# Attention values by seven products in place of eight, with all engines' work ordered by a list scheduler

## The chip, the cores and the metric

The kernel runs on one core of a Trainium2 chip. The core has five engines, each with its own queue of instructions, served in order: TensorE (PE in the profile; its weight loads are PEld), VectorE (DVE), ScalarE (ACT), GpSimd (POOL) and SyncE (SP), which here only issues DMA transfers. Engines wait for each other through semaphores. The metric is the device time of one execution in microseconds.

## The reference

The input is one sequence of 2,048 rows of 256. The first half of the layer is a differential attention between two layer normalisations, the second a feed-forward with Walsh-Hadamard transforms between two more. All is float32. Cut to what matters:

```python
q, k, v = jnp.split(hidden @ Wqkv_w.T + Wqkv_b, ...)   # 16 query heads, 8 key heads, D = 128
p = softmax(causal(q0 @ k0)) - lam * softmax(causal(q1 @ k1))    # 8 pairs of query heads
o = p @ v                                     # v: 4 groups, 256 wide, each for two pairs
o = o * rsqrt(mean(o * o, -1) + EPS) * subln_w * (1 - LAMBDA_INIT)
x = x + layernorm(o.reshape(S, 2048) @ out_w.T + out_b)
h = fwht(layernorm(x) * SU_ug) / 64
h = silu(h @ W_gate.T * s1) * (h @ W_up.T * s2)                  # 1024 wide
x = x + layernorm(fwht(h * SU_dp) / 64 @ W_down.T * s3)
```

The transforms are folded into the three feed-forward weights once, inside the kernel.

## The kernel before, in words

The attention is worked group by group (4 groups of values). A group is cut in units: 8 short ones for the first 1,024 rows (128 queries each, as two halves `subs` of 64) and 16 long ones (64 queries each) for the rest. The 128 rows of a half are its 64 queries for both pairs of heads. Group 0 goes from short to long, the others from long to short.

For each unit:

- `scores` (L268): q times k for both maps, in PSUM tiles of up to 1,024 columns from a pool `ps_s` of three tiles of two banks each. VectorE moves each tile to SBUF with the running minimum (L281 with the causal mask, L286 without).
- `exponentials` (L293) on ScalarE, with the row sums.
- `combine` on VectorE: the factor `cf` (L318, L320) and then e0 + cf * e1 (L325).
- `turn` and `arrive`: VectorE transposes 32x32 blocks (L345), SP writes the result to DRAM (L350) and fetches it back in four pieces (L360), so that keys lie on partitions.
- `values` (L376): for each 128 keys one matmul of 256 columns per half, with the transposed probabilities as weights and v as the moving operand, into a pool `ps_o` of two one-bank tiles. ScalarE copies the sum out (L389) and squares it for the norm (L392); POOL makes the inverse root and scales (`inverse`, L403 to L406).
- `turn_out` and `arrive_out`: the output is transposed in the same way through DRAM (L419, L424, L434), and `project_out` (L443) multiplies it with the output weights; `accumulate` (L453) adds it to `acc` on VectorE.

The projections of q, k (`project_heads`, L181, L200 on ScalarE and L202 on VectorE) and v (`project_values`, L210, L217) use the same three pairs of banks, and so do the feed-forward's hidden products (L706) and its last ones (L741). POOL folds the transforms into the weights (`transform`, L603) between 100 and 505 us.

The order of all this is written by hand: one loop over steps, in which step k issues the scores of unit k, the combine of unit k - 1, the values of unit k - 3 and the output of units before that, with the projections, folds and feed-forward pieces put at named steps (`put`). Each engine's queue follows the order of issue.

Of the kernel before, what the change touches and what calls it, by code (L numbers as in the profile page):

```python
# [10 lines left out]
F32 = mybir.dt.float32  # L11
BF16 = mybir.dt.bfloat16
# [5 lines left out]
P = 128  # L18
# [15 lines left out]
LAG = 3  # L34
# [11 lines left out]
NCOL = 54  # L46


@with_exitstack
def kernel(  # L50
# [18 lines left out]
    ident = const.tile([P, P], F32, name="ident")  # L69
    make_identity(nc, ident)  # L70

    outb_bc = const.tile([P, HID], F32, name="outb_bc")
    make_causal_mask(nc, outb_bc[:, :P], MASKED)
    mask = const.tile([P, 1024], BF16, name="mask")
    nc.gpsimd.memset(mask[:, : 1024 - 64], 0.0)
    for p in range(2):
        nc.gpsimd.tensor_copy(mask[ts(p, 64), 1024 - 64 :], outb_bc[ts(p, 64), ts(p, 64)])
    mhalf = const.tile([P, 4], F32, name="mhalf")
    nc.gpsimd.memset(mhalf, -0.5)

    nlam = const.tile([P, 1], F32, name="nlam")

    acc = const.tile([P, NT, HID], F32, name="acc")

    def rstd_of(pool, src, n, tag):

        st = pool.tile([P, 4, 6], F32, tag="st" + tag, name="st" + tag)
        mv = pool.tile([P, 4, 2], F32, tag="mv" + tag, name="mv" + tag)
        for t in range(n):
            nc.vector.bn_stats(st[:, t, :], src[t] if isinstance(src, list) else src[:, t, :])  # L90
            nc.vector.bn_aggr(mv[:, t, :], st[:, t, :])
        ve = pool.tile([P, 4], F32, tag="ve" + tag, name="ve" + tag)
        nc.vector.tensor_scalar(ve[:, :n], mv[:, :n, 1], EPS, None, ALU.add)
        rstd = pool.tile([P, 4], F32, tag="rs" + tag, name="rs" + tag)
        nc.gpsimd.tensor_tensor(rstd[:, :n], ve[:, :n], mhalf[:, :n], ALU.pow)  # L95
        return mv, rstd
# [12 lines left out]
    x4 = x.rearrange("(b t p) d -> b p t d", p=P, t=4)  # L109

    x2 = x.rearrange("(b t s q) d -> b s q t d", t=2, s=2, q=64)
    outv = out.rearrange("(b t s q) d -> b s q t d", t=2, s=2, q=64)


    with ExitStack() as actx:
        ep = actx.enter_context(tc.tile_pool(name="ep", bufs=3))
        op = actx.enter_context(tc.tile_pool(name="op", bufs=2))
        sm = actx.enter_context(tc.tile_pool(name="sm", bufs=4))
        wop = actx.enter_context(tc.tile_pool(name="wop", bufs=1))
        qkp = actx.enter_context(tc.tile_pool(name="qkp", bufs=1))  # L120
        dram = actx.enter_context(tc.tile_pool(name="dram", bufs=4, space=bass.MemoryType.DRAM))
        ps_s = actx.enter_context(tc.tile_pool(name="ps_s", bufs=3, space=PSUM))
        ps_o = actx.enter_context(tc.tile_pool(name="ps_o", bufs=2, space=PSUM))
        actx.enter_context(tc.manual_schedule())


        qT = [qkp.tile([P, NT, 2, 2, 64], F32, name=f"q{m}") for m in range(2)]
        kT = [qkp.tile([P, S], F32, name=f"k{m}") for m in range(2)]
        vt = qkp.tile([P, NT, HID], F32, name="v")


        xstack = ExitStack()
        xtp = xstack.enter_context(tc.tile_pool(name="xtp", bufs=1, side="right"))
        xnT = xtp.tile([P, NB, 2, 512], F32, name="xnT")
        loaded = {}

        def load_qkv(g, engines, count=4):

            if g not in loaded:
                wq = xtp.tile([P, 2, 1024], F32, tag="wq", name=f"wq_{g}")  # L140
                loaded[g] = wq, xtp.tile([P, 256], F32, tag="vb", name=f"vb_{g}"), list(range(4))
            wq, _, left = loaded[g]
            for _ in range(count):
                k = left.pop(0)
                engines[k % len(engines)].dma_start(wq[:, :, ts(k, 256)], wqkv[4 * g + k])

        def load_vbias(g):
            nc.gpsimd.dma_start(loaded[g][1], vbias[:, ts(g, 256)].to_broadcast([P, 256]))

        wos = {}  # L150

        def load_wo(g):
            wo = wop.tile([P, 2, 2, HID], F32, tag="wo", name=f"wo_{g}")
            nc.gpsimd.dma_start(
                wo.rearrange("p h c o -> p (h c) o"),
                outwT[ts(g, 512), :].rearrange("(k p) o -> p k o", p=P),
            )
            wos[g] = wo

        def scale_wo(g):  # L160
            for c in range(2):
                nc.vector.tensor_scalar(
                    wos[g][:, :, c, :],
                    wos[g][:, :, c, :],
                    colv[:, C_SUBLN + c : C_SUBLN + c + 1],
                    1.0 - LAMBDA_INIT,
                    ALU.mult,
                    ALU.mult,
                )

        def project_heads(g, nb, j2, both=True, n=512):

            wq = loaded[g][0]
            cols4 = ts(nb, n)
            xb, lo = divmod(nb * n, 512)
            nt = n // P
            pp = ps_s.tile([P, 1024], F32, tag="sc", name=f"pp_{g}_{nb}_{j2}_{n}")
            for h in range(2):
                j = 2 * j2 + h
                for c in range(2):  # L180
                    nc.tensor.matmul(  # L181
                        pp[:, 512 * h : 512 * h + n],
                        lhsT=wq[:, c, ts(j, P)],
                        rhs=xnT[:, xb, c, lo : lo + n],
                        start=(c == 0),
                        stop=(c == 1),
                    )
            for h in range(2):
                j = 2 * j2 + h
                col = g * 4 + j if j < 4 else H + g * 2 + j - 4  # L190
                bias = colv[:, C_QKB + col : C_QKB + col + 1]
                src = pp[:, 512 * h : 512 * h + n]
                if j < 4:
                    dst = qT[h][:, ts(nb, nt), :, j2, :].rearrange("d t s q -> d (t s) q")
                    src = src.rearrange("d (t q) -> d t q", q=64)
                else:
                    dst = kT[h][:, cols4]
                scale = -SCALE if j < 4 else 1.0
                if h == 0 or not both:
                    nc.scalar.activation(dst, src, AF.Identity, bias=bias, scale=scale)  # L200
                else:
                    nc.vector.tensor_scalar(dst, src, scale, bias, ALU.mult, ALU.add)  # L202

        def project_values(g, nb):

            wq, vb, _ = loaded[g]
            pp = ps_s.tile([P, 1024], F32, tag="sc", name=f"pv_{g}_{nb}")
            for t in range(4):
                for c in range(2):
                    nc.tensor.matmul(  # L210
                        pp[:, ts(t, 256)],
                        lhsT=xnT[:, nb, c, ts(t, P)],
                        rhs=wq[:, c, 768:1024],
                        start=(c == 0),
                        stop=(c == 1),
                    )
            nc.vector.tensor_tensor(  # L217
                vt[:, ts(nb, 4), :],
                pp.rearrange("p (t e) -> p t e", e=256),
                vb.unsqueeze(1).to_broadcast([P, 4, 256]),  # L220
                ALU.add,
            )


        class Unit:
            def __init__(self, g, i, subs):
                self.g, self.i, self.subs = g, i, subs
                self.ns = len(subs)
                self.nk = i + 1
                self.L = [i * P + 64 * (s + 1) for s in subs]  # L230
                self.at = [a * self.nk * P for a in range(self.ns)]

                self.ng = self.nk if self.ns == 2 else (self.nk + 1) // 2
                self.n = f"{g}_{i}_{subs[0]}"

            def half(self, h):
                return [(h, 0), (h, 1)] if self.ns == 2 else [(0, h)]

            def part(self, m, a):
                return self.es[m][:, self.at[a] : self.at[a] + self.L[a]]  # L240

        def cuts(L):

            if L == 1088 or L == 1600:
                return [704, L - 704]
            return [min(1024, L - c) for c in range(0, L, 1024)]

        def begin(u):
            u.es = [ep.tile([P, S], F32, tag=f"e{m}", name=f"e{m}_{u.n}", bufs=2 + m) for m in range(2)]
            u.mx = sm.tile([P, 4, 2], F32, tag="mx", name=f"mx_{u.n}")  # L250
            u.last = sm.tile([P, 4], F32, tag="last", name=f"last_{u.n}")
            u.d = sm.tile([P, 2, 2], F32, tag="d", name=f"d_{u.n}")

        def scores(u, half):

            for a, m in u.half(half):
                k0 = 2 * a + m
                L = u.L[a]
                e = u.part(m, a)
                best = HIGHEST  # L260
                at = 0
                for c, w in enumerate(cuts(L)):
                    sc = ps_s.tile([P, 2, 512], F32, tag="sc", name=f"sc_{u.n}_{k0}_{c}")
# [65 lines left out]
        def move(u, moved):  # L329

            if u:
                turn(u)
# [695 lines left out]
```

## Time and profile before

| | |
|---|---|
| median of 3 runs | 1438.73 us (1438.65 to 1438.97) |
| the profiled execution | 1438.5 us, span 1436.7 us |
| TensorE busy | 1429.4 us, 99% |
| VectorE busy | 976.7 us, 68% |
| ScalarE busy | 503.8 us, 35% |
| POOL busy | 362.3 us, 25% |
| DMA | 210.76 MB in 501,433 packets, 66.1% of the 16 engines' span on SP's queue |

A line of groups reads: line of the kernel, engine, operation, output from inputs, shape and count, then busy us and mean ns of one, then the engine's idle time just before them and what ended it. A float32 matmul of the program shows as two records.

### The profile page before, as it was taken

The numbers are of one execution on the slowest core, as the hardware profiler recorded it, in microseconds if no ns is written. First come the engines' busy times: TensorE is split into PE (matmuls) and PEld (weight loads), VectorE is DVE, ScalarE is ACT, GpSimd is POOL, SyncE is SP. The second block draws the span as 40 slices with busy tenths as digits, with TensorE's granted clock in tenths as the row PEclk, the third lists the DMA queues.
The fourth block names the chain that finished last, engine by engine and source line by source line (L and its number), as shares of the span: only waits on it lengthen the run. The fifth ranks groups of instructions, "written<-read, shape, count | busy, mean of one in ns | idle before, by whom it ended". The sixth has DMA issues, their size and how long they took to land.

```text
span 1436.7 us, 16896 instructions
## 1 busy us (share of the span) xinstructions
PE 1429.4 (99%) x5436; PEld 1042.5 (73%) x5436; DVE 976.7 (68%) x1789; ACT 503.8 (35%) x1114; POOL 362.3 (25%) x684
## 2 busy tenths in 40 slices
PE   9999999999999999999999999999999999999998
PEld 7567777656766777776677776676777777888887
DVE  6588787847556777544867678445776788656774
ACT  3453433323133334323433334323424445531111
POOL 2037725830028821011111111111111121121110
PEclk9999999999999999999999999999999999999999
DMA  5379899856667897832798887631999999732110
GB/s 147 74 176 201 190 183 222 175 89 139 154 135 145 166 208 179 165 86 62 156 184 178 172 199 168 129 81 52 208 204 192 193 196 188 173 91 81 52 56 18
DMA packets 501433, 210.76 MB, mean 147 GB/s; under 512 B 396032, under 2 KB 499456, under 8 KB 501216
## 3 DMA queue, kind: packets, MB, share of 16 engines
q1 hardware_dynamic: 498128, 200.73, 66.1%
q0 software_dynamic: 2352, 8.26, 2.1%
q8 instruction: 44, 0.72, 0.2%
q10 hardware_dynamic: 864, 0.68, 0.2%
q14 instruction: 45, 0.37, 0.1%
HBM read 111.05 MB, written 98.57 MB: 146 GB/s over the span
## 4 chain that ended last, share of the span: by engine, by line
PE 99%; DMA 0%; DVE 0%; POOL 0%; issue 0%; ACT 0%; POOLq 0%; DVEq 0%
PE po L376 33%; PE sc L268 32%; PE pp L181 11%; PE gu L706 8%; PE pout L443 8%; PE pd L741 4%; PE pv L210 4%; DMA vb<-in_vbias 0%; PE warm L479 0%; DVE v L217 0%; PE pst L508 0%; ACT q L200 0%; POOL lt L536 0%; DVE stx L90 0%; POOL rsx L95 0%
## 5 line engine op out<-in xcount | busy, mean ns | idle before, releaser
L376 PE MATMUL po<-v,pt 128*128 128x256 f32 x2176 | 488.0, 379 | 0.0
L268 PE MATMUL sc<-k,q 128*128 128x512 f32 (+11 forms) x1280 | 477.6, 519 | 0.3 <-DVE last L281 0.2
L376 PEld LDWEIGHTS po<-v,pt 128*128 128x128 f32 x2176 | 426.5, 196 | 66.5 <-issue 18.3
L268 PEld LDWEIGHTS sc<-k,q 128*128 128x128 f32 x1280 | 240.7, 190 | 200.1 <-issue 156.7
L293 ACT ACTIVATE e<-e,last 128x192 f32<-128x192 f32 (+28 forms) x256 | 298.9, 1169 | 199.4 <-DVE last L281 181.8
L286 DVE TENSOR_SCALAR_CACHE_REDUCE e<-sc 128x1024 f32<-128x1024 f32 (+1 forms) x128 | 149.2, 1166 | 153.3 <-PE sc L268 153.3
L389 ACT COPY osb<-po 128x256 f32<-128x256 f32 (+1 forms) x96 | 42.6, 443 | 483.4 <-PE po L376 482.5
L403 POOL TENSOR_TENSOR u<-ss,ed 128x1 f32<-128x1 f32 (+1 forms) x96 | 20.0, 208 | 750.1 <-ACT po L392 749.9
L325 DVE SCALAR_TENSOR_TENSOR e<-e,cf,e 128x64 f32<-128x64 f32 (+31 forms) x128 | 174.1, 1381 | 3.4
L345 DVE STREAM_TRANSPOSE e<-e 128x1536 f32<-128x1536 f32 (+7 forms) x96 | 166.6, 1735 | 7.1
L181 PE MATMUL pp<-xnT,wq 128*128 128x512 f32 (+1 forms) x408 | 170.7, 568 | 0.1
L281 DVE CUSTOM_DVE_ANT_0 e<-sc,mask 128x64 f32<-128x64 f32 (+15 forms) x128 | 89.2, 718 | 79.9 <-PE sc L268 78.7
L181 PEld LDWEIGHTS pp<-xnT,wq 128*128 128x128 f32 x408 | 77.0, 190 | 79.2 <-issue 76.1
L281 DVE CUSTOM_DVE_ANT_0 e<-sc,mask,mx 128x384 f32<-128x384 f32 (+13 forms) x128 | 105.7, 826 | 23.8 <-PE sc L268 8.4
L443 PE MATMUL pout<-wo,oT 128*128 128x256 f32 x512 | 120.9, 379 | 0.0
L443 PEld LDWEIGHTS pout<-wo,oT 128*128 128x128 f32 x512 | 97.3, 190 | 12.8
L719 ACT ACTIVATE hT<-gu,colv 128x256 f32<-128x256 f32 x64 | 26.8, 470 | 120.9 <-PE gu L706 120.8
L706 PE MATMUL gu<-fxnT,wgate 128*128 128x256 f32 x256 | 65.8, 379 | 0.0
L706 PE MATMUL gu<-fxnT,wup 128*128 128x256 f32 x256 | 65.7, 379 | 0.0
L406 POOL TENSOR_SCALAR osb<-osb,f 128x256 f32<-128x256 f32 x128 | 62.5, 488 | 11.9
L404 POOL TENSOR_TENSOR f<-u,mhalf 128x1 f32<-128x1 f32 (+1 forms) x96 | 58.3, 608 | 7.5
L725 DVE SCALAR_TENSOR_TENSOR hT<-gu,colv,hT 128x256 f32<-128x256 f32 x64 | 30.6, 478 | 41.0 <-ACT hT L719 41.0
(100 smaller groups left out, 1079.5 us busy)
## 6 DMA issues: line engine op xcount, KB each, us to landing
dr<-e SPq DMA_DIRECT2D x20, 1024.0 KB, 4.7
pt<-dr SPq DMA_DIRECT2D x80, 256.0 KB, 5.7
dr<-e SPq DMA_DIRECT2D x20, 896.0 KB, 4.5
pt<-dr SPq DMA_DIRECT2D x80, 224.0 KB, 5.1
do<-xo SPq DMA_DIRECT2D x64, 256.0 KB, 3.8
oT<-do SPq DMA_DIRECT2D x256, 64.0 KB, 2.6
dr<-e SPq DMA_DIRECT2D x20, 768.0 KB, 4.3
pt<-dr SPq DMA_DIRECT2D x80, 192.0 KB, 4.5
```

Of the source, the lines that this page charges most:

```text
L181: nc.tensor.matmul(pp[:, 512 * h : 512 * h + n], lhsT=wq[:, c, ts(j, P)], rhs=xnT[:, xb, c, lo : lo + n], start=(c == 0), stop=(c == 1),)
L268: nc.tensor.matmul(src[:, k, :], lhsT=qT[m][:, u.i, u.subs[a]].rearrange("d p q -> d (p q)"), rhs=kT[m][:, lo : lo + w // n], start=True, ...
L281: nc.vector.tensor_tensor_reduce(dst, src, msk, 1.0, best, ALU.add, ALU.min, accum_out=u.last[:, k0 : k0 + 1])
L286: nc.vector.tensor_scalar(dst, src, 1.0, best, ALU.mult, ALU.min, accum_out=least)
L293: nc.scalar.activation(e, e, AF.Exp, bias=u.last[:, 2 * a + m : 2 * a + m + 1], scale=-1.0, accum_out=u.d[:, a, m : m + 1],)
L325: nc.vector.scalar_tensor_tensor(e0, e1, cf[:, a : a + 1], e0, ALU.mult, ALU.add)
L345: nc.vector.transpose(x[:, : 256 * ng].rearrange("p (g c r) -> p r g c", g=ng, r=2), e[:, : 256 * ng].rearrange(order, g=ng, r=2),)
L376: nc.tensor.matmul(u.po[:, ts(a, HID)], lhsT=ptv[:, g, r, :], rhs=vt[:, kc, :], start=(kc == 0), stop=(kc == u.i),)
L404: nc.gpsimd.tensor_tensor(f[:, : u.ns], w[:, : u.ns], mhalf[:, : u.ns], ALU.pow)
L406: nc.gpsimd.tensor_scalar(u.osb[:, a, :], u.osb[:, a, :], f[:, a : a + 1], 16.0, ALU.mult, ALU.mult)
L443: nc.tensor.matmul(u.pout[:, :HID], lhsT=u.oT[:, c, p, :], rhs=wos[u.g][:, p, c, :], start=(p == 0 and c == 0), stop=(p == 1 and c == 1),)
L706: nc.tensor.matmul(ps[:, ts(2 * j + n, 256)], lhsT=ffn[which][:, c, ts(fc, P)], rhs=xnT[:, c, :], start=(c == 0), stop=(c == 1),)
```

## The change

**Values.** The probabilities of one block (256 queries for two pairs of heads, 512 rows) and 256 keys are one item. In the items off the diagonal the product of [2 x 2] blocks is made with seven products in place of eight (Strassen's scheme): POOL makes four sums of blocks of the transposed probabilities per item (`sums`) and, per group, four differences of blocks of v (`vm`). Now v or its differences are the weights and the probabilities the moving operand, so the result comes with the value's 256 entries on partitions and the queries in columns. Diagonal items keep their six products. The products add up in four banks of their own over a block's items; at the end of a block they are collected by ScalarE, VectorE and POOL (`collect_tasks`).

**Output.** Because the result is already turned, `turn_out` and `arrive_out` go. The norm's sum runs over partitions now: squares on ScalarE, a half-sum on POOL, a transpose and a reduction on VectorE, a small round trip through DRAM, a last reduction, and the inverse root on POOL. The factor is applied after the output projection, on ScalarE and VectorE, and POOL adds to `acc`, which starts as the output's bias.

**Evictions.** All q and k evictions are on ScalarE, the pads too.

**PSUM.** Two tiles of two banks (`pair`) serve scores, projections, output projections, the first four feed-forward blocks and all its last products; the four other banks hold the value sums and, once the last block is collected, the hidden products of the last four feed-forward blocks.

**Order.** Every piece of work is a `Task` with an engine, a cost, a key (smaller goes first), dependencies, a latency and perhaps a PSUM slot. `Plan.run` plays the tasks through on costs that are written in the code and issues each when its engine takes it there. Combines and transposes are cut in two for each unit; value fetches go by item.

```diff
+class Plan:
+    def run(self):
+        engines = sorted({t.engine for t in self.tasks})
+        free = dict.fromkeys(engines, 0.0)
...
+        while count < len(self.tasks):
+            best = None
+            for e in engines:
...
+                options = []
+                for k, (_, _, t) in enumerate(sorted(ready[e], key=lambda r: r[:2])):
+                    at = max(first, t.ready, self.room(t)[0])
+                    options.append((at, k, t))
+                    if at == first:
+                        break
...
+    ps_s = ctx.enter_context(tc.tile_pool(name="ps_s", bufs=1, space=PSUM))
+    ps_z = ctx.enter_context(tc.tile_pool(name="ps_z", bufs=1, space=PSUM))
...
+    plan = Plan({"pair": 2, "zb": 4, "sq": 1, "y": 2})
+    def t_pe(n, cols):
+        return n * (cols / 600 + 0.005)
+    def t_dve(cols, fixed=0.15):
+        return fixed + cols / 960
...
+        mixed = add(DVE, t_dve(hi - lo, 0.34), n + MIX + 0.25 * k, c, cf)
+        turned = add(DVE, t_dve(256 * (g1 - g0)), n + MIX + 0.5 + 0.25 * k, t, mixed, u.padded)
...
+        def sums(k):
+            s1, s2, s3, s4 = (b.s[j][:, k, :].rearrange("p (u h c) -> p u h c", u=4, h=2) for k in range(4))
+            a11, a12, a21, a22 = (b.p[j][:, r, k] for r in range(2) for k in range(2))
+            args = (
+                (s1, a21, a22, ALU.add),
+                (s2, s1, a11, ALU.subtract),
+                (s4, a12, s2, ALU.subtract),
+                (s3, a11, a21, ALU.subtract),
+            )[k]
+            nc.gpsimd.tensor_tensor(*args)
...
+            ss.append(add(POOL, 0.8, key + SUM_KEY + 0.01 * k, lambda k=k: sums(k), fetched, room if k == 0 else ss[-1]))
+        def first():
+            p, v = b.p[j], vv[:, j]
+            product(b, 0, 0, v[:, 0, 0, :], p[:, 0, 0], end)
+            product(b, 2, 0, v[:, 1, 0, :], p[:, 0, 1], False)
+            product(b, 2, 256, vm[:, j, 3, :], p[:, 1, 1], False)
+        def second():
+            s = b.s[j]
+            product(b, 1, 0, vm[:, j, 0, :], s[:, 0, :], end)
+            product(b, 0, 256, vm[:, j, 1, :], s[:, 1, :], end)
+        def third():
+            s = b.s[j]
+            product(b, 3, 0, vv[:, j, 1, 1, :], s[:, 3, :], False)
+            product(b, 1, 256, vm[:, j, 2, :], s[:, 2, :], end)
...
+            def cu():
+                nc.vector.tensor_tensor(w["w"][:, 2, :], b.z[0][:, 256:], w["w"][:, 0, :], ALU.add)
+            def co0():
+                nc.vector.tensor_tensor(
+                    b.o[:, 0], b.z[2].rearrange("p (r q) -> p r q", r=2), w["w"][:, 0::3, :], ALU.add
+                )
...
+            def y1(t=t):
+                nc.vector.scalar_tensor_tensor(
+                    r["y", t], r["p"][:, t, HID:], b.f[:, 2 * t + 1 : 2 * t + 2], r["y", t], ALU.mult, ALU.add
+                )
+            def ac(t=t):
+                a = acc[:, 2 * b.i + t, :]
+                nc.gpsimd.tensor_tensor(a, r["y", t], a, ALU.add)
...
+                if many == 2:
+                    r["p"] = pair(where, f"gu_{b}_{k}")
+                else:
+                    r["p"] = ps_z.tile([P, 1, 512], F32, tag=f"z{where}", name=f"gu_{b}_{k}")
```

## The prediction

> **What bounds the kernel now.** I read the page's busy shares, clock row and chain first. TensorE is busy 99% of the span at full clock and carries 99% of the chain; every other engine has slack.
>
> ```profile
> PE 1429.4 (99%) x5436; PEld 1042.5 (73%) x5436; DVE 976.7 (68%) x1789; ACT 503.8 (35%) x1114; POOL 362.3 (25%) x684
> PEclk9999999999999999999999999999999999999999
> PE 99%; DMA 0%; DVE 0%; POOL 0%; issue 0%; ACT 0%; POOLq 0%; DVEq 0%
> ```
>
> Busy is not the same as dense, so next the chain in order of time, and the tail of the timeline.
>
> ```profile
> 298.34 20.60 PE pp L181 x48
> 342.37 6.91 PE po L376 x32
> 1424.18 7.05 PE pd L741 x32
> ...
> 1431.26 0.43 DVE L90 BATCH_NORM_STATS2 stc<-pd 128x6 f32<-128x256 f32 x1 [1.40 <-PE pd L741]
> 1432.83 0.48 DVE L102 SCALAR_TENSOR_TENSOR y<-y,rsc,acc 128x256 f32<-128x256 f32 x1 [0.34 <-POOL rsc L95]
> ```
>
> A program matmul has two records. 16 matmuls of 256 columns take 6.91 us, 0.432 us each; 24 of 512 take 20.60, 0.858 each: 1.67 ns a column and 5 ns a matmul. The program's 2,726 matmuls hold 847,104 columns, so packed densely they take 1,425.5 us. The span is 1,436.7: only 11.2 us are anything else, 1.5 before the first matmul, 5.5 after the last, about 4 in the warm-up and first transposes. So matmul columns are the time, as long as nothing makes TensorE wait. What could make it wait is read from the busy times by stretch (columns: stretch; length, PE, PEld, DVE, ACT, POOL; clock, DMA share, GB/s) and from the waits.
>
> ```profile
> 100.00:200.00 100.00, 100.00 (x382) 73.07 (x381) 81.11 (x128) 38.94 (x86) 65.56 (x105) 1.00 0.89 191
> 1000.00:1200.00 200.00, 200.00 (x750) 144.11 (x749) 154.98 (x254) 82.90 (x165) 30.22 (x75) 1.00 0.97 192
> ...
> DVE e L286 <- PE sc L268: 153.3, 62, 7.8
> POOL u L403 <- ACT po L392: 749.9, 78, 32.4
> ```
>
> VectorE at 81% and DMA at 97% did not cost TensorE anything. VectorE waits for scores, not the reverse.
>
> **Values by seven products.** The order of the built programs counts 1,088 value matmuls of 256 columns before and 976 after: 28 off-diagonal items in each of 4 groups lose one of 8, the diagonal items keep 6. The other matmuls have the same columns. 112 x 0.432 = 48.3 us less. 464 of the 976 read their moving operand in runs of 32 elements, which no row shows. The nearest row is the old value matmul, which loads its weights at a step of two yet keeps 0.432 us like the contiguous projections: I take 0. Below it could hardly fall; above, 6 ns a record is what the strided weight load costs (196 against 190 ns), 464 x 2 x 6 ns = 5.6 us.
>
> **VectorE.** Removed: 64 output transposes (45.1), 40 projection evictions that move to ScalarE (29.7), 64 additions into acc that move to POOL (26.8): 101.6 us. Added: 56 collecting additions of 256 columns at 0.42 (as L453) and 56 of 512 at 0.70 (nearest the 0.74 eviction), 63 us; per block a transpose 0.70, a reduction about 0.69 and a small one 0.2, 51 us; 64 scaled additions at 0.48, 31; the combine and the transpose cut in more pieces, 64 more of each at 0.22 and 0.17, 25. Sum +170 - 102 = +68, so 1,045 us, 75% of a 1,390 us span. That alone hides.
>
> **POOL, and what it does to VectorE.** POOL loses 155 us (L406, L404, L403, pads) and gains 448 sums, 64 differences of values and 64 additions into acc of 256 columns, at about 0.8 as the fold's (461); 60 additions of 512 at twice 0.73 (87), 64 short copies at 0.23 and 32 powers at 0.61 (35): about 580. It goes from 362 to some 790 us, 57%. Rows of the fold's additions, of cf, and of one width of the combine while POOL folds (234 to 300 us) and while it does not (600 to 1200):
>
> ```profile
> L603 POOL TENSOR_TENSOR t_up<-t_up x56: 608/727/2040, 113.2 to 182.1; 128x256 f32<-128x256 f32 x56
> L320 DVE SCALAR_TENSOR_TENSOR cf<-d,nlam,r x96: 219/221/2282, 34.1 to 1270.9; 128x1 f32<-128x1 f32 x64, 128x2 f32<-128x2 f32 x32
> ...
> L325 DVE SCALAR_TENSOR_TENSOR e<-e,cf,e 128x1920 f32<-128x1920 f32 x1 | 2.8, 2764 | 0.0
> ...
> L325 DVE SCALAR_TENSOR_TENSOR e<-e,cf,e 128x1920 f32<-128x1920 f32 x2 | 4.4, 2219 | 0.1
> ```
>
> The two engines hold each other up. Over the three folding stretches (251 us, POOL busy 195, 78%) 24 combines take 0.33 us more than equal widths in the quiet one, and 21 cf 0.34 more than 0.22. After, 192 combines and 96 cf: 63 + 33 = 96 us at 78% POOL, 69 at 57%, of which 15 are in the old trace: +54. VectorE comes to about 1,100 us, 79%.
>
> The Trainium skill, "SBUF — State Buffer", section "Who interferes with whom", has the rule: a VectorE instruction with two SBUF inputs and a GpSimd instruction that reads SBUF take turns, and the later one fully blocks until the first is done. By it a wait is bounded by one POOL operation of 0.8 us; the cf of 2.28 us shows more. By the rule alone (288 instructions, half an operation each, 57% of the time) it would be 66 us in place of 69, and the forecast would not move.
>
> Where VectorE has room this costs nothing. It has none early: between TensorE's 60th and 200th dense microsecond the new order holds VectorE instructions worth 135 us by their rows, in 15 units, and blocking adds 1.0 us a unit (one cf, two combines): 150 in 140. I take +10; ends 0 (the excess is caught up around it) and 27 (every blocked microsecond of the attention, 54, half on the path).
>
> **Scores in two tiles.** Scores, projections and the early feed-forward rotated over three pairs of banks; now over two, the value sums having four banks of their own. For each reuse of a pair I take the matmul time in the order between the last matmul into the old tile and the first into the new, less the rows of its evictions (1.29 us for 1024 columns). Before: 490 reuses, median margin 6.2 us, 5 under 0.35. After: 442, median 2.55, 15 below zero, 27 under 0.35, 69 under 1.0. The handshake between the engines also takes time: at most 0.71 us, since the old order has margins of 0.71 between 100 and 200 us, where TensorE is 100% busy. I take half, 0.35: the shortfalls then sum to 1.7 us before and 10.7 after, +9. Ends: 4.2 with no handshake (+2), and 41 (+39) if each eviction comes 0.65 us later still, as when VectorE is in the middle of a combine or a transpose of some 1.2 us. Queued behind a stalled score are the value matmuls; what waits for them is only TensorE itself.
>
> **The rest.** ScalarE: loses 115 us of copies and squares and 8 table loads (10), gains 27 of evictions, 50 of collecting and scaling, 36 of squares, 29 of pads, 32 DMA issues: about 525, under TensorE. SyncE: 901 issues become 1,096 (192 writes at a median 0.38, 576 fetches at 0.51, the rest at about 0.45), some 515 us of issuing; the output's round trip through DRAM (64 writes, 256 fetches, 32 MB) goes, 224 tiny ones for the norms come, and 166 MB land in place of 191. What hides the value fetches is their lead: an item's 128 KB pieces land in 3.3 us (row of that size) and are asked for some units ahead; without it, the slowest fetch row less this one, 5.7 - 3.3 = 2.4 us, for each of 32 blocks, 77. POOL's sums run up to two items ahead; without it, 0.83 for every second of 112 items, 46. Both I cost at nothing, because stretches with DMA at 97% and with POOL at 78% show no TensorE wait. The tail: the last block's two halves share one tile, so 16 matmuls end before either statistics chain; two chains of 0.43 + 0.18 + 0.15 + 0.48 and two 0.48 make 3.6 us against 2.05 from 1431.26: +1.5.
>
> **Sum.** Against the profiled execution's 1,438.5 us (1,436.7 and 1.8 around it): 1,438.5 - 48.3 + 1.5 + 10 + 9 = 1,410.7. It lay 0.2 under the median of the runs, so 1,411.
>
> **Rivals.**
> *Full gain.* Planned slack absorbs blocking and handshakes: 1,438.7 - 48.3 + 1.5 = 1,392, or 1,391 without the old 1.7. For it: 81% VectorE with no wait from 100 to 200 us. Against: the 15 negative margins.
> *VectorE becomes the bound (slower).* Its evictions come late behind blocked combines while only one other pair is free. It decides when the stalls pass 46.8 us: at about 1.1 us more lateness than the rows at each reuse. At the upper ends, 39 + 27 in place of 19, it gives 1,458. For it: 79% mean load with gaps of 2.55 us. Against: the value matmuls between scores give cover that a wait can use up first.
> *The strided moving operand is slow.* 5.6 us by the weight rows gives 1,417; a quarter more per matmul, 464 x 0.107 = 50 us, gives 1,461. Nothing in the trace speaks for it.
> *Late sums or fetches* eat the gain: 46 us gives 1,457; 27 of them would already make it no change. Against it: the lead of two items.
>
> **How the numbers follow.** Forecast (stalls of 5 to 40 us in place of 19) 0.56; full gain 0.17; VectorE-bound 0.16; strided operand 0.05; late sums or fetches 0.06. The range runs from 1,391, the floor of the full gain, to 1,446, which leaves out the worse part of the last three, some 0.15. The likeliest case alone: 1,397 to 1,432. Faster by over 0.2% (below 1,435.9; that is about what a measurement tells from no change): 0.56 + 0.17 + 0.03 = 0.76. Within it 0.04, slower 0.20.
>
> **What would show it.** Value matmuls at 0.432 us in runs of the chain, or longer where strided; PE busy near 1,400 with idle behind DVE evictions, most between 60 and 200 us; the means of the cf and combine rows up by a third of a microsecond; VectorE near 1,100 and POOL near 790; small waits of PE for POOL's sums or for DMA. Wrong if PE waits for sums or fetches by tens of microseconds, if VectorE passes 90%, or if those matmuls stretch.

## The result and the profile after

The changed kernel takes 1453.99 us (median of 4 runs, 1449.56 to 1455.53), against 1438.85 us for the kernel before on the same chips: 1.01 times as long, with a 95% interval of 1.0078 to 1.0122. The forecast was 1,411, the range ended at 1,446: the sign was wrong. The profiled execution took 1453.65 us, with a span of 1451.9.

The page of the changed kernel begins so (busy time in us, share of the span and instructions; then the busy tenths of TensorE and its granted clock in 40 slices of 36 us):

```profile
span 1451.9 us, 17509 instructions
PE 1399.4 (96%) x5212; PEld 990.8 (68%) x5212; DVE 1064.5 (73%) x2060; ACT 527.2 (36%) x1050; POOL 782.0 (54%) x1011
...
PE   8779999999999999999999999999999989999998
PEclk9989999999999999999999999999999989999999
```

TensorE has 224 records (112 matmuls) fewer, but its busy time falls by 30.0 us and not by the 48 they are worth, and it stands idle for 52.5 us of the span in place of 7.3. The slices say where: the second and third (36 to 109 us) and the 33rd (1,162 to 1,198 us). Its waits, as total us, times and longest:

```profile
PE z L254 <- DMA pt<-dr: 24.2, 3, 16.0
PE sc L254 <- DVE last L724: 5.4, 7, 2.2
PE z L254 <- DVE o L1020: 2.8, 1, 2.8
PE po L254 <- DVE e L728: 2.5, 3, 1.2
```

The value matmuls (z) wait for fetched probabilities (pt), and 16.0 of the 24.2 us are one wait. It stands alone in the timeline, here with what SyncE issued before it (start, duration, what; idle before and its cause in brackets), first TensorE, then SyncE:

```profile
64.19 1.13 PE L254 MATMUL sc<-k,q 128*128 128x288 f32 x4
81.29 3.37 PE L254 MATMUL z<-pt,v 128*128 128x256 f32 x8 [15.97 <-DMA pt<-dr]
```

```profile
37.80 3.60 SPq L483 DMA_DIRECT2D acc<-in_outb  x1
63.92 1.29 SPq L1081 DMA_DIRECT2D fin<-de  x2
65.31 1.20 SPq L838 DMA_DIRECT2D dr<-e  x2
76.11 1.91 SPq L881 DMA_DIRECT2D pt<-dr  x4
```

At 37.8 us the output's bias, one row of 1 KB, is spread over the 2 MB of `acc`. The list of transfers (KB each, median us to landing) has it as the longest of all:

```profile
pt<-dr SPq DMA_DIRECT2D x576, 128.0 KB, 3.7
...
acc<-in_outb SPq DMA_DIRECT2D x1, 2048.0 KB, 37.2
```

It lands at about 75 us, and the fetch that the next value matmuls need goes out at 76.1. What comes between is slow too. These are transfers that go out from 40 to 60 us and, the second row, from 55 to 85 us:

```profile
de<-ed ACTq DMA_DIRECT2D x2, 2.0 KB, 20.4
dr<-e SPq DMA_DIRECT2D x2, 128.0 KB, 10.2
```

SyncE serves its queue in order. Its next piece after the fill (fin) needs the first of the 2 KB transfers (de) that ScalarE sends for the norm, and waits 22.5 us for it; only then do the two writes of probabilities (dr) go out, at 65.3 us, and the fetch waits for them. The second hole shows in the stretches (length, busy us of PE, PEld, DVE, ACT, POOL, granted clock, DMA share, GB/s):

```profile
70.00:80.00 10.00, 0.00 (x0) 0.00 (x0) 0.00 (x0) 0.00 (x0) 0.00 (x0) 0.52 0.46 92
80.00:90.00 10.00, 8.71 (x29) 6.55 (x30) 2.52 (x7) 3.06 (x8) 8.50 (x16) 0.79 0.68 162
1170.00:1180.00 10.00, 4.18 (x12) 2.83 (x12) 8.42 (x14) 4.20 (x11) 4.00 (x7) 0.65 0.89 125
```

Around 1,170 us the three feed-forward weights come back from DRAM (1 MB each). Between 70 and 80 us every engine stands still: they wait for this chain, which stands behind one transfer.

To compare kernels I use one number from the traces, called **lost time**: the time between the starts of successive matmul records, less 0.83 ns a column and 2.5 ns a record (1.67 and 5 a matmul, the dense pitch of the prediction). It was 5.9 us before and is 68.2 after. With the tail (6.8 us after the last matmul against 5.5) this closes the account of the span: 1436.7 - 48.3 + 62.3 + 1.3 = 1452.0. By stretches, with the main experiments below (in each kernel's own time; the edges lie in quiet places). The table holds one execution of each kernel; executions of one kernel differ by up to 7 us (1432.2 to 1439.4 for the small fill), and the stretch from 1,120 to 1,260 us reads 14.6 to 18.3 us in three kernels that do the same there (after, small fill, no fold). So 2 to 4 us in one stretch show nothing by themselves.

| us | before | after | small fill | no weights fetched | no fold | small fill, no combine | repaired |
|---|---|---|---|---|---|---|---|
| 0-40 | 4.1 | 9.1 | 8.9 | 8.6 | 8.6 | 8.9 | 9.2 |
| 40-100 | 0.4 | 18.5 | 2.3 | 18.6 | 19.7 | 1.5 | 1.7 |
| 100-240 | 0.2 | 8.5 | 8.6 | 9.8 | 6.9 | 1.4 | 12.1 |
| 240-440 | 0.0 | 2.3 | 1.3 | 2.4 | 1.3 | 1.3 | 1.4 |
| 440-520 | 0.0 | 4.9 | 4.7 | 4.5 | 3.0 | 2.9 | 0.0 |
| 520-1120 | 0.5 | 6.3 | 6.9 | 6.1 | 6.9 | 5.3 | 6.1 |
| 1120-1260 | 0.5 | 16.8 | 18.3 | 6.7 | 14.6 | 14.2 | 10.4 |
| 1260-end | 0.1 | 1.8 | 1.8 | 1.8 | 1.8 | 1.8 | 1.8 |
| sum | 5.9 | 68.2 | 52.8 | 58.4 | 62.8 | 37.2 | 42.6 |

### The profile page after: what moved, and what is told of

Its sections match the earlier page's. It is cut to its first block, busy times and chain, and to the rows that moved or that the text cites. A ratio compares the mean times of both kernels' runs of the same rounds, so it can differ in the third digit from the quotient of the medians.

```text
span 1451.9 us, 17509 instructions
## 1 busy us (share of the span) xinstructions
PE 1399.4 (96%) x5212; PEld 990.8 (68%) x5212; DVE 1064.5 (73%) x2060; ACT 527.2 (36%) x1050; POOL 782.0 (54%) x1011
## 3 DMA queue, kind: packets, MB, share of 16 engines
q10 hardware_dynamic: 5744, 1.01, 0.4%
## 4 chain that ended last, share of the span: by engine, by line
PE 79%; DVE 11%; DMA 5%; SPq 3%; issue 2%; POOL 1%; ACT 0%; POOLq 0%; ACTq 0%; DVEq 0%
PE sc L254 24%; PE z L254 23%; PE pp L254 11%; PE gu L254 8%; PE po L254 6%; PE pd L254 4%; PE pv L254 3%; DVE e L724 2%; DVE e L821 2%; DVE e L829 2%; DMA pt<-dr 2%; SPq L881 2%; DMA de<-ed 2%; DMA dr<-e 1%; DVE e L728 1%
## 5 line engine op out<-in xcount | busy, mean ns | idle before, releaser
L254 PE MATMUL sc<-k,q 128*128 128x512 f32 (+10 forms) x1280 | 496.6, 520 | 7.0 <-DVE last L724 5.4
L759 ACT ACTIVATE e<-e,last 128x192 f32<-128x192 f32 (+28 forms) x256 | 299.5, 1170 | 455.1 <-DVE last L724 420.8
L943 POOL TENSOR_TENSOR sum<-pt 128x256 f32<-128x256 f32 x224 | 177.7, 795 | 192.3 <-PE z L254 138.5
L821 DVE SCALAR_TENSOR_TENSOR e<-e,cf,e 128x768 f32<-128x768 f32 (+9 forms) x192 | 218.0, 1157 | 2.1
L254 PE MATMUL z<-pt,v 128*128 128x256 f32 x704 | 180.4, 387 | 27.4 <-DMA pt<-dr 24.2
L254 PE MATMUL z<-sum,vm 128*128 128x256 f32 x672 | 183.8, 383 | 0.7 <-POOL sum L943 0.7
L254 PEld LDWEIGHTS z<-pt,v 128*128 128x128 f32 x704 | 135.7, 194 | 70.6 <-issue 37.7
L829 DVE STREAM_TRANSPOSE e<-e 128x768 f32<-128x768 f32 (+3 forms) x192 | 179.1, 957 | 0.1
L254 PEld LDWEIGHTS z<-sum,vm 128*128 128x128 f32 x672 | 129.3, 193 | 39.9 <-issue 19.1
L728 DVE TENSOR_SCALAR_CACHE_REDUCE e<-sc 128x1024 f32<-128x1024 f32 (+7 forms) x116 | 124.9, 1090 | 42.1 <-PE sc L254 33.5
L254 PE MATMUL po<-wo,o 128*128 128x256 f32 x512 | 116.2, 380 | 2.8 <-DVE e L728 2.5
L254 PEld LDWEIGHTS z<-sum,v 128*128 128x128 f32 x352 | 67.1, 191 | 32.2 <-issue 20.7
## 6 DMA issues: line engine op xcount, KB each, us to landing
acc<-in_outb SPq DMA_DIRECT2D x1, 2048.0 KB, 37.2
```

Source lines behind the costliest of these rows:

```text
L254: nc.tensor.matmul(o, lhsT=lhsT, rhs=rhs, start=start, stop=stop, **kw)
L728: nc.vector.tensor_scalar(dst, src, 1.0, best, ALU.mult, ALU.min, accum_out=to)
L759: nc.scalar.activation(e, e, AF.Exp, bias=u.last[:, 2 * a + m : 2 * a + m + 1], scale=-1.0, accum_out=u.d[:, a, m : m + 1],)
L821: nc.vector.scalar_tensor_tensor(e0, e1, o["cf"][:, a : a + 1], e0, ALU.mult, ALU.add)
L829: nc.vector.transpose(y.rearrange("p (g b k q) -> p k g b q", g=g1 - g0, b=4, k=2), e.rearrange("p (g k b q) -> p k g b q", g=g1 - g0, b=4 ...
L943: nc.gpsimd.tensor_tensor(*args)
```

## The experiments

Two theories. **T** (transfers): the gain is lost to DMA traffic that the forecast put at nothing, the 2 MB fill and the return of the feed-forward weights. **V** (VectorE): it is lost to evictions that come late because VectorE, held up by POOL, is full and only two score tiles are left; the transfers only stand beside it. Unless said otherwise each engine's order is that of the changed kernel.

### The fill, and where it is issued

The first kernel loads 128 KB (the bias on 128 partitions once) and adds it with the first group's addition into `acc`:

```diff
-        nc.sync.dma_start(acc, outb.unsqueeze(1).to_broadcast([P, NT, HID]))
+        nc.sync.dma_start(outb_bc, outb.to_broadcast([P, HID]))
...
-                nc.gpsimd.tensor_tensor(a, r["y", t], a, ALU.add)
+                nc.gpsimd.tensor_tensor(a, r["y", t], a if b.g else outb_bc, ALU.add)
```

> The bias of the output projection is loaded once as 128 KB and added in the first group's additions, in place of a 2 MB broadcast into acc; the order of all engines stays. Transfers are the cause (theory T): the 2 MB transfer, 37.2 us from issue to landing, holds the write and the fetch that the first value products wait for; without it the 16.1 us stall near 81 us shrinks to 1 to 3 us, the halved clock after it goes (1.6 us), and the time falls by 15 to 20 us, to 1434 to 1439. VectorE is the cause (theory V): work is only moved between waits, and the time falls by less than 6 us.

Measured: 1436.58 us (10 runs, 1432.2 to 1439.43), ratio to before 0.9981, interval 0.9971 to 0.9991. 17 us, as T has it; lost time between 40 and 100 us falls from 18.5 to 2.3. TensorE's waits are now

```profile
PE z L255 <- DMA pt<-dr: 6.6, 2, 4.5
PE sc L255 <- DVE last L725: 5.5, 8, 1.9
PE po L255 <- DVE e L729: 3.1, 3, 1.7
```

The second keeps the 2 MB and moves them from SyncE's queue to POOL's (`nc.sync` becomes `nc.gpsimd` in the first line above; there they go out at 28.8 us in place of 37.8):

> The same 2 MB broadcast, but issued from POOL's queue in place of SP's, everything else in place. If SP's later transfers stand behind it in the same queue, they no longer do, and the time falls nearly as in the small fill, by 12 to 20 us. If the transfer takes the DMA engines or one DRAM row itself, the stall stays: less than 4 us gained. Theory V: less than 4 us too.

Measured: 1449.56 us (4 runs), ratio 1.0074 (1.0059 to 1.0089): only 4.4 us better. The transfer and TensorE's two longest kinds of wait:

```profile
acc<-in_outb POOLq DMA_DIRECT2D x1, 2048.0 KB, 32.8
```

```profile
PE z L254 <- DMA pt<-dr: 10.1, 4, 4.7
PE pp L254 <- DVE last L724: 9.8, 2, 9.1
```

The transfer holds up others whichever queue it is in. Its place in SyncE's queue is not what makes it costly.

The third keeps queue, place and 2 MB, and reads 2,048 different rows in place of one row 2,048 times:

```diff
-        nc.sync.dma_start(acc, outb.unsqueeze(1).to_broadcast([P, NT, HID]))
+        nc.sync.dma_start(acc, x.rearrange("(t p) d -> p t d", p=P))
```

> The changed kernel with its 2 MB fill read from 2 MB of distinct rows (x) in place of one 1 KB row read 2,048 times; place, queue, size and order are the same, and acc begins with x in place of the output's bias. If the 37.2 us of that transfer come from its size (2 MB at this place), it takes over 25 us still and the stall near 81 us stays over 10: 1,448 to 1,454. If they come from the single row as a source, 2 MB at the 300 GB/s that the fetches of probabilities reach take about 7 us, and the stall falls under 3: 1,437 to 1,441.

Measured: 1433.69 us (one run), lost time between 40 and 100 us 3.1, and

```profile
acc<-in_x SPq DMA_DIRECT2D x1, 2048.0 KB, 12.2
```

Slower than the 7 us I expected, in a kernel a little faster than the expected 1,437 to 1,441, but a third of 37.2, and the stall is gone. So it is neither the 2 MB nor the queue but the one row, read 2,048 times. The packets in the trace say the same: those of 1 KB take 138 ns in the mean while the fill from one row runs, 54 from distinct rows, and 55 where the row is read 128 times (small fill). The 3 us to the small fill lie within that kernel's own spread.

### The return of the weights

Here the three weight tiles are set to a constant and not fetched (the feed-forward works with other weights):

```diff
-            nc.sync.dma_start(
-                ffn[which][ts(a, 32)].rearrange("k (n w) -> k n w", w=64),
-                ffn["dr", which][:, :, :, a, :].rearrange("g b k w -> k (g b) w"),
-            )
+        nc.gpsimd.memset(ffn[which], 0.01)
```

> The three folded feed-forward weights are filled with a constant on chip in place of 3 MB fetched in twelve transfers near 1145 to 1174 us; the feed-forward is then computed with these constants. Theory T: the fetches of probabilities and ScalarE's wait of 6.6 us for the last weight go; of the 16.8 us lost between 1160 and 1240 us 8 to 14 are gained, 1440 to 1446. Theory V: VectorE is the cause there (busy 115 of 150 us from 1100 to 1250), under 3 us gained.

Measured: 1444.17 us (one run), 9.8 less, all of it in the last third: 16.8 us of lost time between 1,120 and 1,260 become 6.7. Of the waits there only VectorE's are left:

```profile
PE z L254 <- DVE o L1020: 2.7, 1, 2.7
PE sc L254 <- DVE last L724: 0.7, 1, 0.7
PE po L254 <- DVE last L724: 0.6, 1, 0.6
```

What about them is costly: their place in SyncE's queue, their coming all at once, or their 12,288 packets of 256 B? Four kernels, all with the small fill. In the first the planner sends a quarter of a weight at a time, 4 us apart, in SyncE's queue, and the weights are written to DRAM in quarters too:

```diff
-        w_ok[which] = add(SP, 2.1, 91, lambda which=which: arrive_weights(which), opened, lat=8.0)
+        for a in range(4):
+            step = add(SP, 0.6, 91, lambda which=which, a=a: arrive_weights(which, a), step, lat=4.0)
```

> The version with the 128 KB fill, and with the feed-forward weights written in four DMAs each and fetched one quarter at a time, 4 us apart by the plan, with the sign pass of ScalarE planned 12 us later. The planner is unchanged, but the order after 1,130 us moves with the new DMAs. If late transfers are the loss (theory T): the waits of the value matmuls for fetched probabilities at 476, 1,152 and 1,162 us (2.8, 2.1 and 4.5 in the run with the small fill) and most of what else is lost between 1,120 and 1,240 us (18.4 in all) go: 1,436.6 - 3 - (8 to 14) = 1,420 to 1,427. If that stretch is slow because VectorE or GpSimd is full there (theory V), moving the weights saves under 4: 1,432 to 1,438.

Measured: 1437.52 us (10 runs), ratio 0.9993 (0.9983 to 1.0002): no gain. The 4.7 us between 440 and 520 went, with the cut writes; between 1,120 and 1,260 the lost time did not fall (22.1 after 18.3). The twelve pieces went out over 67 us there (1,125.8 to 1,192.6); a wider spacing was not tried. The second sends the same quarters from ScalarE's queue (`nc.scalar` and `add(ACT, ...)` in the lines above):

> As the version with the small fill and the spread weights, but the twelve quarter fetches of the feed-forward weights are issued from ScalarE's queue instead of SyncE's; ScalarE has 12 more issues of some 0.6 us and stays under half busy there. Theory Q (SyncE's queue is the loss: the weights stand between the fetches of probabilities, and one that must wait, like the 14.4 us one at 1,132, holds what is behind it): the stretch from 1,120 to 1,240 us falls from 19.2 us of lost time to the 7 of the run without weights: 1,437.5 - 12 = 1,424 to 1,430. Theory E (the 3 MB themselves take the DMA engines or the landing time from the fetches, whatever queue issues them): under 5 us are gained, 1,432 to 1,438.

Measured: 1435.8 us (9 runs), ratio 0.9983 (0.9973 to 0.9993), 20.7 us of lost time in the stretch: 1.7 us better in place of 12, as theory E has it. But the move does not take the weights out of SyncE's way. In the trace, the transfers of both queues take eight semaphores in turn (100 to 107), and an issue starts only when the last transfer on its semaphore has landed, whichever engine sent that. So SyncE still stands 28.7 us for weight quarters that ScalarE issued (its fetches of probabilities 11.7 for `wup`, 2.8 for `wgate` and 5.8 for `wdown`), and theory Q is not settled by this kernel. The trace has the way from a transfer to TensorE in three timelines, SyncE, VectorE and TensorE:

```profile
1168.72 5.91 SPq L1383 DMA_DIRECT2D fxnT<-df  x4
1174.74 0.39 SPq L839 DMA_DIRECT2D dr<-e  x1
1175.23 2.77 SPq L882 DMA_DIRECT2D pt<-dr  x4
1178.11 0.42 SPq L839 DMA_DIRECT2D dr<-e  x1
```

```profile
1171.84 0.61 DVE L725 CUSTOM_DVE_ANT_0 e<-sc,mask 128x448 f32<-128x448 f32 x1
...
1182.62 0.62 DVE L725 CUSTOM_DVE_ANT_0 e<-sc,mask 128x448 f32<-128x448 f32 x1 [10.16 <-DMA dr<-e]
```

```profile
1183.40 5.88 PE L255 MATMUL po<-wo,o 128*128 128x256 f32 x16 [8.27 <-DVE last L725]
```

SyncE spends 5.9 us on a fetch for the feed-forward, 4.3 of them waiting for a quarter of `wdown` that ScalarE sent at 1,167.1. The writes of finished probabilities (dr) stand behind it; the second goes out at 1,178.1 and lands at 1,182.5, where VectorE has waited 10.2 us for the buffer that it empties, and TensorE waits 8.3 us for the score tile that VectorE would have emptied. A "wait for VectorE" is a late write here. The DMA engines are busy meanwhile (a share of 0.87 or more in each ten microseconds); the list of transfers from 1,160 to 1,190 us shows

```profile
DMA packets 16775, 6.10 MB, mean 203 GB/s; under 512 B 14211, under 2 KB 16772, under 8 KB 16772
```

So the next kernel changes the number of packets. The weights lie in DRAM so that a partition's 8 KB are one run; the 256 B runs move to the writes, in 16 small transfers per weight between 165 and 520 us, where the order also changes a little:

```diff
+            ffn["dr", which] = dram.tile([4, 32, 8, 4, 64], F32, tag="dw", name=f"dw_{which}")
...
+        nc.sync.dma_start(ffn[which], ffn["dr", which].rearrange("a k g b w -> (a k) (g b w)"))
```

> As the version with the small fill, but the feed-forward weights lie in DRAM so that each of the 128 rows of a fetch is one run of 8 KB: three DMAs of 1 MB from SyncE's queue in place of twelve with 12,288 runs of 256 B; the runs of 256 B move to the writes, which are cut into 16 small DMAs per weight between 200 and 480 us. Sign passes are planned 12 us later. If the number of 256 B packets is what holds the fetches of probabilities up between 1,120 and 1,240 us (theory P: 12,288 packets are some 20 us of all 16 DMA engines at the rate of the stretch at 1,160 to 1,190 in the run before, 16,775 packets in 30 us), the lost time there falls from 18 to 19 us to 5 to 9: 1,436 - (9 to 14) = 1,422 to 1,428. If the bytes or the place in SyncE's queue hold them up (theory Q), it stays over 14: 1,432 to 1,438. The writes may give back 1 to 4 us before 480.

Measured: 1431.03 us (4 runs), ratio 0.994 (0.992 to 0.996). It misses the expected 1,422 to 1,428 for two reasons: 6 us are given back between 100 and 240 us, where the writes go out (8.6 becomes 14.9), and the stretch itself falls from 18.3 to 12.6, between the 5 to 9 of theory P and the "over 14" of Q. The same from ScalarE's queue, with the first feed-forward inputs at a lower priority:

> As the run with rows of 8 KB, with the three weight fetches issued by ScalarE and the feed-forward input of the first blocks sent and fetched at a lower priority of the plan, behind the last writes of probabilities. Theory P (packets): the same as with rows of 8 KB from SyncE's queue, within 3 us. Theory Q (place in SyncE's queue): 8 us or more better than that run: 1,420 to 1,428.

Measured: 1428.89 us (4 runs), ratio 0.9934 (0.992 to 0.9949); 9.7 us in the stretch, and no wait of TensorE for pt left there:

```profile
PE sc L255 <- DVE last L725: 3.1, 2, 2.4
PE z L255 <- DVE o L1021: 2.4, 1, 2.4
PE po L255 <- DVE last L725: 1.2, 1, 1.2
```

The four together, as lost time from 1,120 to 1,260 us: 256 B runs 22.1 from SyncE's queue and 20.7 from ScalarE's, 8 KB runs 12.6 and 9.7, against 6.7 with nothing fetched. The step to 8 KB runs gains 6 to 11 us, by whether one sets it against the small fill (18.3) or the spread quarters. It changes two things at once, though: 12,288 runs become 384, and twelve transfers become three, which also take fewer of the shared semaphores; that it is the packets is likely and not shown by itself. The queue's 1 to 3 us lie within the spread, and SyncE still waits 11.7 us for ScalarE's weights in the last kernel (which also holds the lower priority, not tried by itself).

### The fold and the combine

The 208 additions by which POOL folds the transforms into the weights are left out (other weights again), on the changed kernel:

```diff
     def transform(which, n, j, q):
+        return
```

> The 208 additions on POOL that fold the transforms into the weights are left out (the weights are used unfolded), all else in place; POOL falls by about 150 us, all of it before 470 us. Theory V: combines and cf no longer wait for POOL there, VectorE falls by about 15 us, and most of the 12 us of waits for evictions between 85 and 470 us go: 6 to 12 us gained. Theory T: the stall near 81 us and the late ones stay, 0 to 5 us gained.

Measured: 1448.29 us (one run), 5.7 less, just below V's 6 to 12 and above T's 0 to 5: spread over many places, as the table shows, and the stall near 81 us stays. The four runs of the changed kernel differ by 6.0 us, so one run does not decide here. Against the small fill, VectorE's combine is left out but for the first block:

```diff
-                nc.vector.scalar_tensor_tensor(
-                    e0, e1, o["cf"][:, a : a + 1], e0, ALU.mult, ALU.add
-                )
+                if u.g == 0 and u.i == 0:
+                    nc.vector.scalar_tensor_tensor(
+                        e0, e1, o["cf"][:, a : a + 1], e0, ALU.mult, ALU.add
+                    )
```

> The version with the 128 KB fill, with VectorE's combine of the two maps left out for all units but the first block of the first group (some 217 of its 218 us; the values are then formed from the first map alone); all engines keep their order. If the score, projection and output tiles wait for VectorE because it is full (theory V: 13.2 + 6.5 + 5.6 = 25.3 us in the run with the small fill, of which some 6 lie in the start-up), these fall to under 10, and the writes of the probabilities come earlier too: 1,436.6 - (15 to 25) = 1,412 to 1,422. If these waits are consequences of late transfers or of the order alone (theory T), under 8 go: 1,429 to 1,437.

Measured: 1422.71 us (one run), 13.9 less than the small fill; lost time falls by 15.6, of it 7.2 between 100 and 240 us (8.6 to 1.4) and 4.1 between 1,120 and 1,260. Just outside V's bound in time, but not T's "under 8": a loaded VectorE is a real second term of some 15 us. It is not the first: the transfers hold some 31.

### Put together

The kernel called repaired in the table is the version with 8 KB rows from ScalarE's queue, with the planner told the old cost of a write so that TensorE's order is again that of the changed kernel:

```diff
-            fold = add(SP, 1.2, key + 3, lambda which=which, b=b: keep_weights(which, b), fold, lat=4.0)
+            fold = add(SP, 0.3, key + 3, lambda which=which, b=b: keep_weights(which, b), fold, lat=4.0)
```

> As the run with rows of 8 KB from ScalarE's queue, with the planner told the old 0.3 us for each piece of a weight write, so that TensorE's order is that of the changed kernel throughout. In the run before, the stretch from 100 to 240 us lost 12.6 us against 8.6 in the order of the changed kernel. Theory O (that order is the cause): 4 us less, 1,423 to 1,427. Theory S (the 16 writes delay SyncE there, whatever the order): no gain, 1,427 to 1,431.

Measured: 1428.05 us (5 runs, 1426.01 to 1429.33), ratio 0.9923 (0.9909 to 0.9937). It beats both kernels, by 10.7 and 25.9 us, but not the run before it: the order was not what cost between 100 and 240 us (12.1 us still). What is left as a difference there is the 16 writes. The last four stand in SyncE's queue ahead of writes of probabilities whose data VectorE had ready by 189.7 us; the one that VectorE waits for goes out at 194.6. SyncE, then VectorE:

```profile
189.77 2.76 SPq L1277 DMA_DIRECT2D dw_up<-x_up  x4
192.65 0.54 SPq L839 DMA_DIRECT2D dr<-e  x1
...
194.61 1.78 SPq L839 DMA_DIRECT2D dr<-e  x3
```

```profile
197.74 1.23 DVE L729 TENSOR_SCALAR_CACHE_REDUCE e<-sc 128x1024 f32<-128x1024 f32 x1 [2.71 <-DMA dr<-e]
```

The same without the combine:

> The run above with VectorE's combine left out for all units but the first block of the first group (values from the first map alone). Theory T (late transfers and a full VectorE are separate terms that add): 12 to 16 us less than the run above, TensorE's lost time some 25 to 28 us. If the remaining losses of both kinds cover each other, under 8 less.

Measured: 1422.2 us (one run); lost time 36.5, only 6 less than with the combine. The two kinds of loss cover each other in part, against T: 6.1 us lie between 160 and 200 us, where the weight writes hold VectorE up with or without combines (it waits 3.8 us for one dr there).

## Why the prediction was wrong, step by step

**The step that failed** stands under "The rest": "Both I cost at nothing, because stretches with DMA at 97% and with POOL at 78% show no TensorE wait." For POOL's sums it held: TensorE waits 0.7 us for them in all. For fetches it did not. Of the 62.3 us of new lost time, 16 go with the 2 MB fill, 10 with the return of the weights and 4.7 with an uncut weight write at 480 us: about 31. The rival "late sums or fetches" named the right wait and was given 6 in 100, but its 1,457 lies near the measured 1,454 by luck: its price was a small delay at each of 32 blocks or at every second item, and what came was three waits for fetches, of 16.0, 5.0 and 3.1 us, and late writes, behind transfers that the price did not hold. The argument carried a share of busy time from the old order over to the new one. The old kernel has DMA at 92% from 1,120 to 1,260 us and loses 0.5 us there (columns as before):

```profile
1120.00:1260.00 140.00, 140.00 (x573) 109.07 (x572) 109.55 (x232) 70.41 (x167) 25.71 (x63) 1.00 0.92 188
```

and the new one loses 16.8 us there at a lower share:

```profile
1120.00:1260.00 140.00, 130.14 (x510) 98.33 (x509) 104.09 (x232) 56.97 (x138) 76.29 (x100) 0.95 0.89 167
```

What differs is how the transfers come. The old order sends the twelve weight pieces one by one, about 12 us apart, from 1,026.6 to 1,161.0 us, and only the last four fall into this stretch; the new one sends all twelve from 1,145.6 to 1,168.7. It is not that the new order fetches later in general: from the landing of an item's fetch to the first matmul on it lie 17.3 us in the median, 8.3 before. But a stretch without waits did not mean room. The old order's shortest leads, beside its last weight pieces at 1,156 and 1,165 us, are 0.5 us. I read fetches "asked for some units ahead" and "the lead of two items" of the sums as cover, and never asked what stands in SyncE's queue within that lead. No run gives the new order the old spacing, so that the bunching is what costs is argued and not shown. And the fill, which the description of the change names, has no line in the working: it is one of 1,096 issues "at about 0.45" and 2 of 166 MB.

**Matmul pitch and values by seven**: right. The strided matmuls are those that read the fetched probabilities themselves (z<-pt, 928 records); POOL's sums (z<-sum) are contiguous. In both, most records take 379 ns and start 216 ns apart; the means differ by 4 ns because more of the first kind are slow ones, such as the eight at 81.29 us. So the 0 for the strided operand held (busy us, mean ns; idle before):

```profile
L254 PE MATMUL z<-pt,v 128*128 128x256 f32 x704 | 180.4, 387 | 27.4 <-DMA pt<-dr 24.2
L254 PE MATMUL z<-pt,vm 128*128 128x256 f32 x224 | 67.8, 385 | 0.0
L254 PE MATMUL z<-sum,vm 128*128 128x256 f32 x672 | 183.8, 383 | 0.7 <-POOL sum L943 0.7
```

The 48.3 us are there; the account above closes with them.

**VectorE and POOL by themselves**: 1064.5 us against "about 1,100", 782 against "some 790". Blocking was overestimated. Counted above the shortest instruction of the same shape, combines and cf took 56 us more after and 16 before: +40, where the sum has +54. For cf alone:

```profile
L810 DVE SCALAR_TENSOR_TENSOR cf<-d,nlam,r 128x1 f32<-128x1 f32 (+1 forms) x96 | 35.9, 374 | 3.4
```

A cf takes 374 ns in the mean against 0.22 undisturbed: 0.15 us more, 15 us in 96, where 33 us at 78% of POOL scaled to 54% give 23 (0.24 each). The Trainium skill, "SBUF — State Buffer", section "Who interferes with whom", by which the wait is bounded by one POOL instruction, gives as an estimate half a sum (0.8 us) in 54% of cases, 0.22 each: a little nearer than my row from the folding stretch, still above the measured 0.15.

**VectorE full between 60 and 200 us, +10**: right in size and place; 7.2 of 8.6 us there go without the combine. That takes out the combine's own 218 us as well as its waits for POOL, so that blocking is the reason is not shown; without the fold 1.6 of 8.5 go.

**Two score tiles, +9**: not isolated, since no third tile can be added without taking banks from the value sums. What stays with neither fill nor combine, outside the start-up and the return of the weights, is 13 us (1.5, 1.4, 1.3, 2.9, 5.3 and 1.8, less 1.2 before), 2.9 of them the weight write at 480: at most some 10. The two VectorE terms, 19 together, met at most 25: these 10 and the 15 that go with the combine.

These shares overlap, so they need not add up: with the transfers repaired, leaving out the combine saves 6 us in place of 14.

**Missed besides**: the start-up, 9.1 against 4.1 us, where the new order begins its scores at 26 us in place of 18. **Tail**: +1.3 against +1.5 (the terms printed there add up to 3.4 us and not 3.6, so to +1.4; likewise 96 us at 78% make 70 at 57%, not 69: neither matters).

## What to carry to other kernels

A busy share with no wait beside it shows that the old order had lead enough, nothing more: list every transfer of 1 MB or more in the new order, with what is queued behind it and which buffer waits for that. Sending it from another engine's queue is no way round while both queues share completion semaphores: look at SyncE's own waits before and after. A list scheduler knows only the latencies written into it, and a transfer planned at 12 us that takes 37 stops five engines. Before a rewrite is judged by its algorithm, take away its one-off transfers in a trial: here nearly 2% of the time lay in two of them.

## What the runs showed of the hardware that was not expected

- A 2 MB transfer whose source is one row of 1 KB took 37.2 us (32.8 from POOL's queue), one from 2,048 rows 12.2 us. Transfers beside it were slow too: 2 KB took 20.4 us and 128 KB 10.2, against 6.1 and 1.8 in the kernel with distinct rows.
- TensorE's granted clock fell to half 5 us into its 16 us stall and stayed there until 84.1 us, 3 us after its return (0.52 in the profile from 70 to 80 us, 0.79 from 80 to 90). The eight value records at 81.29 take 3.37 us, where eight such records take 1.89 later in the same run (at 1,143.5 us). Of the 68.2 us of lost time 18.0 lie between records with no idle between them, against 5.2 before, and 7.8 of these 18.0 in four stretches at half clock after the start-up (none of the 5.2). So a stall costs more than its length.
- 3 MB in 256 B runs cost TensorE 6 to 11 us more than in 8 KB runs at the same place, with the same bytes (the number of transfers fell too, from twelve to three). From 1,160 to 1,190 us 16,775 packets, mostly under 512 B, kept the DMA engines busy with only 203 GB/s.
- In these programs the transfers of SyncE and ScalarE take eight completion semaphores in turn, and an issue waits for the last transfer on its semaphore: SyncE stood 28.7 us for weights that ScalarE had sent.
